# Moving the value steps, the gated biases and the output stores of a quantised cross-attention kernel, and cutting its scale loads into eight

## The chip, the core and the metric

The kernel runs on one core of a Trainium2 chip. The metric is device time in microseconds for one execution. Engines in the views: PE (matrix products), PEld (its weight loads), DVE (vector), ACT (scalar), POOL (GpSimd) and SP, which computes nothing here and issues most DMAs. An engine works through its instructions in order; so does SP through the DMAs that it issues.

## What is computed

A gated cross-attention block and a gated feed-forward block, with quantised arithmetic (rounding left out here):

```python
def xattn(x, cond):                      # 2048 query tokens, 4096 keys, C = 512, 16 heads of 32
    q = (x @ Wq + bq) * scale            # per head; integers of 8 bits, a step for each token and head
    k, v = split(cond @ Wkv + bkv)       # k: a step for each key and head; v: one step for each column
    attn = softmax(q @ k.T)              # then 8 bits, a step for each row
    return (attn @ v) @ Wp + bp
x = x + tanh(g_xattn) * xattn(layernorm(x), ctx)
x = x + tanh(g_ffn) * ffn(layernorm(x))  # 512 -> 2048 -> 512, ternary weights, 8-bit tokens, + b1, + b2
```

A value's step belongs to a column of `v`, which is a column of a head's output; it may be applied to the values, to the output of the head, or to the rows of `Wp` that this output meets. A bias `bp` times `tanh(g_xattn)` can be added to `x` before the product is.

## The kernel before, in words

There are three stretches. The first, the projections, makes integers of queries, keys and the first group of values, and leaves them and the key scales in DRAM (`q4d`, `k4d`, `skd`). It runs over 48 tiles of 128 rows; `extra[i]` holds what is done beside tile `i` (the ternary weights, the gates by `gates`, `tg1` and `tg2`).

The second, the attention, has 256 steps: 16 heads of 16 query tiles, the last two heads interleaved by four tiles. A step `i` has three chunks of keys (1536, 1536, 1024). PE makes the scores of a chunk (L726), DVE multiplies them by the key scales `skb` of the head and keeps their maximum (L735); POOL joins the maxima and makes a bias (L750, L752); ACT makes the exponentials as bytes in one of three buffers `r` (L755); SP transposes the bytes by DMA into `pT` (L769); POOL turns them into numbers that PE can read (L789, two casts a step); PE multiplies them by the values (L805); every four steps ACT empties the accumulator into `o` (L816) and issues the store of it to DRAM (L817). The score buffers are three until step 237 and two from there on, since the third holds then the output weight `wp_sb` and the vectors `bp` and `b2` (`load_for_ffn`).

Order is written out by hand. `plan[i, n]` lists what is issued after chunk `n` of step `i`; at the end of step `i` SP gets the transpose of step `i - 2` and then the loads of the next head. A head's data come in eight pieces (`load_piece`): 0 and 1 are the keys (L256), 2 and 3 the key scales in halves of 2048 keys, broadcast to 128 partitions, 1 MB each (L249), 4 to 7 the queries (L256). Before, pieces 0 to 7 of head `h + 1` are issued at the even steps of head `h`, and in head 0 at the steps `LATE`. Three more groups of values are made beside the heads (`plan_group`, from steps 3, 64 and 129): products from `cTd` (L646, L652, L661), stores and fetches by `vtd` (L674, L678), then transposes by DMA (L278). `value_scale` makes the steps `sv` of a group.

The third stretch is the output projection and the feed-forward block over tiles of 128 tokens. Its first tiles are started inside the last heads by `at_unit(i, n, ...)`: `projection_step` multiplies the output weight by the value steps (L282), `vector_for_ffn` the vectors by the gates (L191), `bias_x` adds the gated `bp` to the tokens (L1005), `wide_step` spreads the softmax steps (L1018), `first_project` multiplies (L1408). All of L191, L282 and L1005 is on POOL.

Of the kernel before, what the change touches and what calls it, by code (L numbers as in the profile page):

```python
# [11 lines left out]
F32 = mybir.dt.float32  # L12
# [5 lines left out]
AF = mybir.ActivationFunctionType  # L18
ALU = mybir.AluOpType
# [4 lines left out]
P = 128  # L24
# [5 lines left out]
INT_STEP = 2.0**-24  # L30
# [3 lines left out]
def flamingo_kernel(  # L34
# [31 lines left out]
    nc = tc.nc  # L66
    x = x.flatten_outer_dims()
    cond = cond.flatten_outer_dims()
    out = out.flatten_outer_dims()
    NQ, C = x.shape  # L70
    NK = cond.shape[0]
    H, HD = 16, 32
    INNER = w1.shape[0]
    QT, KT, CC, IC = NQ // P, NK // P, C // P, INNER // P
    HPG = P // HD
# [3 lines left out]
    def row(v, width):  # L79
        return v.rearrange("(a w) -> a w", a=1).broadcast_to([P, width])  # L80
# [79 lines left out]
    }  # L160
    b1r = third[:, at_vecs + 8 * C : at_vecs + 8 * C + 2 * INNER].bitcast(BF16)
    b1d = dram.tile([3, INNER], BF16, name="b1d")

    def load_b1(pool):
        bf = pool.tile([IC, P], F32, name="bf", bufs=1)
# [11 lines left out]

    def load_for_ffn():
        nc.sync.dma_start(wp_sb, wp.rearrange("(c p) n -> p c n", p=P))
        for name, v in (("bp", bp), ("b2", b2)):  # L180
            nc.sync.dma_start(vecs[name], row(v, C))
        for r in range(2):
            for a in range(3):
                at = r * HD + 3 * a
                nc.sync.dma_start(
                    b1r[at : at + 3, :].rearrange("p (m n w) -> p m n w", n=2, w=512)[:, :, r, :],
                    b1d.rearrange("p (m n w) -> p m n w", n=2, w=512)[:, :, r, :],
                )

    def vector_for_ffn(name, tg):  # L190
        nc.gpsimd.tensor_scalar(vecs[name], vecs[name], tg, 0.0, ALU.mult, ALU.add)  # L191

    def key_tile(n):

# [44 lines left out]
    def load_piece(h, n):  # L239
# [17 lines left out]
            dst[:, :, a : a + KB], src[a : a + KB, h * P : (h + 1) * P]  # L257
        )

    def value_scale(g, vmx):  # L260

        nc.vector.tensor_reduce(
            sv[:, g : g + 1], vmx, AX.X, ALU.max, apply_absolute_value=True
        )
        nc.vector.tensor_scalar(
            sv[:, g : g + 1], sv[:, g : g + 1], 1.0 / 127.0, 1e-8, ALU.mult, ALU.max
        )
        nc.vector.reciprocal(isv[:, g : g + 1], sv[:, g : g + 1])
# [8 lines left out]
            vqs[g] = vqp.tile([P, KT, P], F16, name="vq")  # L277
        nc.sync.dma_start_transpose(vqs[g][:, j * VB : (j + 1) * VB, :], vh)  # L278

    def projection_step(g):  # L280

        nc.gpsimd.tensor_scalar(  # L282
            wp_sb[:, g, :], wp_sb[:, g, :], sv[:, g : g + 1], 1.0 / INT_STEP, ALU.mult, ALU.mult
        )

    def integers(pool, f, scale):

# [21 lines left out]
    with tc.tile_pool(name="pw", bufs=1) as pw, tc.tile_pool(  # L309
# [215 lines left out]
            partial(nc.sync.dma_start, bq_sb, row(bq, C)),  # L525
        ]
        extra[5].append(load_gates)
        extra[45].append(gates)
        extra[4] += [partial(nc.vector.tensor_scalar, bq_sb, bq_sb, QSCALE, None, ALU.mult)]
        for j in range(8):  # L530
            extra[6 + 2 * j].append(partial(piece_load, j))
# [9 lines left out]

        extra[22].append(ffn_load)
        extra[23].append(lambda: parts_of_b1(pieces.pop(0), wr))
        LASTK = KT + QT - END - 1
        for k, n in ((-6, 0), (-3, 4), (-1, 5), (1, 1), (1, 2), (1, 3)):
            extra[LASTK + k].append(partial(load_piece, 0, n))
# [82 lines left out]

    VW = 256  # L630
    NV = NK // VW
    LATE = (4, 6, 8, 10, 11, 12, 13, 14)
    VALUES = {3: (1, 4, 2), 64: (2, 66, 0), 129: (3, 131, 0)}

    def plan_group(g, u0, dense):
        wv_g = wvs.next()
        vmx = fs.tile([P, KT // VB], F32, name="vmx")
        state = {}

        def start(j):  # L640
# [27 lines left out]

        def store(b):
            v = state.pop(("v", b))  # L670
            nc.vector.tensor_reduce(
                vmx[:, b : b + 1], v, AX.X, ALU.max, apply_absolute_value=True
            )
            nc.sync.dma_start(vtd[g][:, b * VB * P : (b + 1) * VB * P], v)  # L674

        def fetch(j):
            vt = vts.next()
            nc.sync.dma_start(vt, vtd[g][:, j * VB * P : (j + 1) * VB * P])  # L678
            state["vt", j] = vt

        def integer(j):
            state["vi", j] = value_integers(vis.next(), g, state.pop(("vt", j)))

        def cast(j):
            state["vh", j] = vhs.next()
            nc.vector.tensor_copy(state["vh", j], state.pop(("vi", j)))

        def turn(j):
            values_by_key(state.pop(("vh", j)), g, j)

        nc.sync.dma_start(wv_g, values_weight(g))
        load(0)
        for j in range(NV):
            u = start(j)
            v = start(j + 1) - 1
            for c, place in enumerate(((u, 2), (u + 1, 0), (v, 0) if v > u + 1 else (v, 1), (v, 2))):
                plan[place].append(partial(product, j, c))
            if j + 1 < NV:
                plan[u, 1].append(partial(load, j + 1))
            plan[v, 2].append(partial(leave, j))  # L700
            if (j + 1) * VW % (VB * P) == 0:
                plan[v + 1, 1].append(partial(store, j * VW // (VB * P)))
        u = start(NV)
        plan[u + 1, 0].append(partial(value_scale, g, vmx))
        for j in range(KT // VB):
            n = u - 1 + 2 * j
            plan[n + 1, 1].append(partial(fetch, j))
            plan[n + 3, 0].append(partial(integer, j))
            plan[n + 4, 2].append(partial(cast, j))
            plan[n + 5, 1].append(partial(turn, j))  # L710
# [65 lines left out]
    def plan_values(i, h, tg):  # L776
# [36 lines left out]

        def leave():
            o = ar.tile([P, P], F32, name="o", bufs=2)
            nc.scalar.copy(o, acc)  # L816
            nc.scalar.dma_start(  # L817
                ods[tg][h * HD : (h + 1) * HD, :].rearrange("d (c q) -> c d q", c=TG), o
            )

# [170 lines left out]
        return range(g * GT, (g + 1) * GT)  # L991

    def load_x(t):
        nc.sync.dma_start(X[t], x[t * P : (t + 1) * P, :])

    def load_o(t):
        o = fm["o"].next()
# [16 lines left out]
    def wide_step(t):  # L1014

        step_w = fm["step_w"].next()
        step = ff.pop(("step", t))
        nc.scalar.copy(step_w, step.unsqueeze(2).to_broadcast([P, H, HD]))  # L1018
        ff["step_w", t] = step_w

    def bias_y(g):
# [374 lines left out]
    def at_unit(i, n, *fs_):  # L1396
        plan[i, n].extend(fs_)
# [5 lines left out]
    def first_project(t, n):  # L1403
# [6 lines left out]
            start=(k == 0), stop=(k == NG - 1),  # L1410
        )

    for j in range(8):
        a = j * INNER // 8
        at_unit(
            199 + 3 * j, 1,
            partial(
                nc.sync.dma_start_transpose,
                w1T[:, :, a : a + INNER // 8],
                w1q[a : a + INNER // 8, :],  # L1420
            ),
        )
    at_unit(TWO + 2, 0, load_for_ffn)
    at_unit(TWO + 3, 2, partial(vector_for_ffn, "bp", tg1))
    for g in range(NG):
        at_unit(TWO + 4 + g // 2, 1, partial(projection_step, g))
    at_unit(TWO + 7, 1, partial(vector_for_ffn, "b2", tg2))
    at_unit(
        TWO + 7, 1,
        partial(  # L1430
# [5 lines left out]
    for t in range(2):  # L1436
        at_unit(240, t, partial(load_x, t))
        at_unit(241, 1, partial(load_o, t))
        at_unit(242 + t, 0, partial(bias_x, t))
    at_unit(241, 0, partial(steps_x, 0))  # L1440
    for t, u in ((0, 242), (1, 248)):
        at_unit(u - 1, 2, partial(wide_step, t))
# [15 lines left out]
    with tc.manual_schedule():  # L1458
        nc.vector.memset(less, -128.0 * INT_STEP)
        nc.vector.memset(ones_h, 1.0)  # L1460
        for i in range(len(steps)):
            h, t = steps[i]
            for n in range(len(CHUNKS)):
                scores(i, n)

                if n == 0 and i in VALUES:
                    plan_group(*VALUES[i])
                if n == 0 and i:
                    exps(i - 1)
                for run in plan.pop((i, n), ()):  # L1470
                    run()
            if i > 1:
                turn_exps(i - 2)
            if h == 0:
                if t in LATE:
                    load_piece(1, LATE.index(t))
            elif h + 2 < H and t % 2 == 0:
                load_piece(h + 1, t // 2)
            if 0 <= i - PAIR < TG:
                for n in ((0, 4, 2), (1, 3), (5,), (6, 7))[i - PAIR]:  # L1480
                    load_piece(H - 1, n)
# [142 lines left out]
```

## Time and profile before

| | us |
|---|---|
| median of three runs (lowest, highest) | 1709.2 (1708.43, 1712.97) |
| the profiled execution: own time | 1714.34 |
| the profiled execution: span of its instructions | 1712.5 |
| busy: DVE / PE / ACT / POOL | 1566.7 / 1366.1 / 1343.1 / 1283.7 |
| L735 on DVE, 768 instructions | 806.0 + 362.6 |
| L789 on POOL, 506 casts | 944.1 |
| L755 on ACT, 256 exponentials | 673.1 + 300.3 |
| first and last L735 start | 236.7 and 1452.8 |

Times are counted from the start of the span. In a timeline a line has the start, the duration, the engine with its line number, the operation and the tile written and read; a bracket gives the idle time before it and what ended that. "SPq" and "ACTq" are the queues that issue DMAs: the duration is that of the issue, not of the transfer. In a list of waits the numbers are the sum, the count and the longest. Idle time of an engine that is not the bottleneck costs nothing.

### The profile page before, as it was taken

What the parts mean: (1) busy time and instruction counts of PE and PEld (TensorE: products, weight loads), DVE (VectorE), ACT (ScalarE), POOL (GpSimd) and SP (SyncE); (2) the same over time, 40 slices, a digit from 0 to 9 for tenths busy, and PEclk for the clock granted to TensorE, in tenths of its full rate; (3) what the DMA queues carried; (4) which work ended last, traced back from release to release, by engine and by line L of the source; (5) the groups of instructions that cost most, each with busy time, mean ns of one, the idle gap of its engine ahead of it and who ended that gap; (6) DMA issues with size and microseconds to landing.
All of it is one profiled execution on the core that took longest, in us unless ns stands there. A gap on an engine that the chain in (4) does not pass through costs nothing. (4 is left out here: it accounts for less than half of the span.)

```text
span 1712.5 us, 31561 instructions
## 1 busy us (share of the span) xinstructions
PE 1366.1 (80%) x12174; PEld 592.1 (35%) x12174; DVE 1566.7 (91%) x2205; ACT 1343.1 (78%) x988; POOL 1283.7 (75%) x1315
## 2 busy tenths in 40 slices
PE   8999968889966899886678998766666577789986
PEld 4444423333322333332233333222222233434432
DVE  5787889999999999999989999999999989578998
ACT  2443468888889798888978888898887877679987
POOL 0001226889999899999988999999999998656645
PEclk9999975555555555555555556555555555889998
DMA  6767969999999999999999999989999776613325
GB/s 208 274 248 249 300 189 225 194 211 212 181 200 189 212 189 207 208 197 202 173 208 185 227 181 215 202 171 198 165 198 179 151 140 130 169 50 87 89 53 117
DMA packets 736331, 315.92 MB, mean 184 GB/s; under 512 B 658034, under 2 KB 703670, under 8 KB 729782
## 3 DMA queue, kind: packets, MB, share of 16 engines
q1 hardware_dynamic: 727414, 309.19, 83.4%
q10 hardware_dynamic: 8736, 4.72, 1.1%
q8 instruction: 95, 1.56, 0.4%
q14 instruction: 54, 0.44, 0.1%
q0 software_dynamic: 32, 0.01, 0.0%
HBM read 110.15 MB, written 40.12 MB: 88 GB/s over the span
## 5 line engine op out<-in xcount | busy, mean ns | idle before, releaser
L789 POOL CAST rT<-pT 128x2048 int16<-128x2048 uint8 x506 | 944.1, 1892 | 28.9 <-DMA pT<-r 7.5
L735 DVE CUSTOM_DVE_ANT_0 s<-ps_s,skb 128x1536 f32<-128x1536 f32 x531 | 806.0, 1574 | 21.1 <-PE ps_s L726 13.0
L755 ACT ACTIVATE r<-s,nb,sq 128x4096 uint8<-128x4096 f32 x177 | 673.1, 3803 | 135.6 <-POOL nb L752 77.1
L726 PE MATMUL ps_s<-kT,qT 32*128 32x512 bf16 x2048 | 463.7, 593 | 245.7 <-DVE m L735 232.1
L735 DVE CUSTOM_DVE_ANT_0 third<-ps_s,skb 128x1536 f32<-128x1536 f32 (+1 forms) x237 | 362.6, 1574 | 5.5 <-PE ps_s L726 3.2
L755 ACT ACTIVATE r<-third,nb,sq 128x4096 uint8<-128x4096 f32 x79 | 300.3, 3802 | 46.7 <-POOL nb L752 34.0
L726 PEld LDWEIGHTS <-qT 32*128 32x128 bf16 x2048 | 95.4, 99 | 578.0 <-issue 571.1
L805 PE MATMUL acc<-rT,vq 128*32 128x128 f16 x8192 | 265.1, 307 | 33.3 <-ACT o L816 25.2
L805 PEld LDWEIGHTS <-vq 128*32 128x32 f16 x8192 | 196.8, 137 | 147.0 <-issue 105.1
L652 PE MATMUL vacc<-fx 128*128 128x256 f32 x384 | 231.4, 706 | 7.7 <-ACT fx L661 6.7
L750 POOL TENSOR_SCALAR m<-m 128x1 f32<-128x1 f32 x256 | 91.8, 359 | 67.8 <-DVE m L735 61.2
L472 POOL TENSOR_SCALAR nsq<-sq 128x16 f32<-128x16 f32 x16 | 3.2, 203 | 171.9 <-DVE sq L291 171.9
L652 PEld LDWEIGHTS vacc<-fx 128*128 128x128 f32 x384 | 94.9, 306 | 91.3 <-issue 79.2
L431 PE MATMUL kacc<-wk_sb,cT 128*128 128x512 f32 x256 | 117.7, 603 | 0.0
L752 POOL TENSOR_SCALAR nb<-m,nsq 128x1 f32<-128x1 f32 x256 | 67.8, 265 | 23.9
L1117 PE MATMUL ph<-fx,skb 128*128 128x512 bf16 x256 | 64.2, 396 | 0.1
L431 PEld LDWEIGHTS kacc<-wk_sb,cT 128*128 128x128 f32 x256 | 47.1, 194 | 47.6 <-issue 47.0
L735 DVE DVE_READ_ACCUMULATOR2_ANT m<- 128x1 f32 x768 | 62.7, 82 | 0.0
L431 PE MATMUL qacc<-wq_sb,xT 128*128 128x512 f32 x128 | 59.4, 608 | 0.1
L460 DVE TENSOR_TENSOR f<-kacc,bk_sb 128x512 f32<-128x512 f32 x32 | 22.0, 689 | 31.1 <-PE kacc L431 30.1
L300 ACT COPY cT<-tr 128x512 f32<-128x512 f32 x32 | 18.6, 580 | 34.8 <-PE tr L299 34.6
L360 POOL TENSOR_SCALAR wi<-wt 128x512 bf16<-128x512 int32 (+1 forms) x32 | 21.7, 704 | 31.5 <-ACT wt L356 19.3
(233 smaller groups left out, 1370.1 us busy)
## 6 DMA issues: line engine op xcount, KB each, us to landing
skb<-skd SPq DMA_DIRECT2D x32, 1024.0 KB
fx<-cTd SPq DMA_DIRECT2D x48, 512.0 KB
wt<-in_L_ffn_w_dram SPq DMA_DIRECT2D x16, 1024.0 KB
in<-in_ctx_dram SPq DMA_DIRECT2D x32, 256.0 KB
cTd<-cT SPq DMA_DIRECT2D x8, 1024.0 KB
q4d<-rows4q SPq DMA_DIRECT2D x16, 512.0 KB
vtd<-fx SPq DMA_DIRECT2D x24, 256.0 KB
fx<-vtd SPq DMA_DIRECT2D x24, 256.0 KB
```

The lines of the kernel that those rows point to most:

```text
L360: nc.gpsimd.tensor_scalar(wi[:, a : a + w4], wt.bitcast(I32)[:, a : a + w4], 1.0, -1.0, ALU.min, ALU.max)
L431: nc.tensor.matmul(acc, tT[:, c, :], wk_sb[c] if kind == "k" else wq_sb[:, c, :], start=(c == 0), stop=(c == CC - 1),)
L460: nc.vector.tensor_tensor(f, acc, bk_sb, ALU.add)
L652: nc.tensor.matmul(state["acc"], wv_g[:, c, :], state["cT", j][:, c, :], start=(c == 0), stop=(c == CC - 1),)
L726: nc.tensor.matmul(ps_s[:, b * KB - k0 : (b + 1) * KB - k0], qT[rows, 0, t * P : (t + 1) * P], kT[rows, 0, a * KB : (a + 1) * KB], start=True,
L735: nc.vector.tensor_tensor_reduce(s[:, k0 : k0 + w], ps_s[:, :w], skb[:, k0 : k0 + w], 1.0, -3.0e38, ALU.mult, ALU.max, m3[:, n : n + 1],)
L750: nc.gpsimd.tensor_scalar(m, m3[:, 0:1], m3[:, 1:2], m3[:, 2:3], ALU.max, ALU.max)
L752: nc.gpsimd.tensor_scalar(nb, m, nsq[:, t, h : h + 1], LN255, ALU.mult, ALU.add)
L755: nc.scalar.activation(r.rearrange("p (n two) -> p two n", two=2), s.rearrange("p (two n) -> p two n", two=2), AF.Exp, bias=nb, scale=sq[: ...
L789: cast(spreads[k][:, 2 * u : 2 * u + 2, :, :] .bitcast(I16) .rearrange("p a (two b) q -> p a two (b q)", two=2), pTs[u][:, :, k * NW : (k ...
L805: nc.tensor.matmul(acc[c * HD : (c + 1) * HD, :], vq[:, kb, h % HPG * HD : (h % HPG + 1) * HD], rT[:, c, b, :], start=(k == 0 and b == 0), ...
L1117: nc.tensor.matmul(ph[:, n, :], xqT[:, c, tok], w1T[:, c, at : at + 512], start=(c == 0), stop=False,)
```

## The change

Five things are done.

1. The steps of the values no longer go into the output weight (`projection_step` is gone). They are stored to `svd` and loaded as a column for each head into `svr`, by one store and four loads for each of the four groups, and `leave` applies them when ACT empties the accumulator. The constant `1 / INT_STEP` goes into `wide_step`.
2. The products of `bp` and `b2` with the gates, and the sum of the first two tiles of tokens with the gated `bp`, are made on POOL in the projections and kept in DRAM (`gbd`, `xbd`); `load_for_ffn` and `load_x` read those, and `vector_for_ffn` and two calls of `bias_x` are gone. The gates are made at tile 9 in place of tile 45.
3. The store of `o` is issued by SP at step `i + 9` for the first 13 heads, in place of ACT at step `i + 8`; for the last three it stays with ACT.
4. The key scales of a head come in eight loads of 512 keys (256 KB each).
5. These and the six other pieces are issued at steps 0 to 11 of a head (`PIECES_AT`, `SCALES_AT`), in head 0 at steps 4 to 15. The loads of the last head are unchanged.

```diff
+    gbd = dram.tile([2, C], F32, name="gbd")
+    xbd = dram.tile([2 * P, C], F32, name="xbd")
...
     def load_for_ffn():
         nc.sync.dma_start(wp_sb, wp.rearrange("(c p) n -> p c n", p=P))
-        for name, v in (("bp", bp), ("b2", b2)):
-            nc.sync.dma_start(vecs[name], row(v, C))
+        for k, name in enumerate(("bp", "b2")):
+            nc.sync.dma_start(vecs[name], gbd[k : k + 1, :].broadcast_to([P, C]))
...
-    def vector_for_ffn(name, tg):
-        nc.gpsimd.tensor_scalar(vecs[name], vecs[name], tg, 0.0, ALU.mult, ALU.add)
...
+    def load_scales(h, k):
+        a = k * KB
+        nc.sync.dma_start(
+            heads[h][1][:, a : a + KB], skd[h : h + 1, a : a + KB].broadcast_to([P, KB])
+        )
...
-    def projection_step(g):
-        nc.gpsimd.tensor_scalar(
-            wp_sb[:, g, :], wp_sb[:, g, :], sv[:, g : g + 1], 1.0 / INT_STEP, ALU.mult, ALU.mult
-        )
+    svr = keep.tile([P, H], F32, name="svr")
+    svd = dram.tile([NG, P], F32, name="svd")
+
+    def store_scale(g):
+        nc.sync.dma_start(svd[g : g + 1, :].rearrange("a p -> p a"), sv[:, g : g + 1])
+
+    def load_scale(g):
+        for c in range(HPG):
+            nc.sync.dma_start(
+                svr[c * HD : (c + 1) * HD, g * HPG : (g + 1) * HPG],
+                svd[g : g + 1, :].rearrange("a (h d) -> (a d) h", d=HD),
+            )
...
-        extra[45].append(gates)
+        extra[9].append(gates)
...
+        def bias_load():
+            wt = wr.tile([P, INNER], F32, name="wt")
+            biased.append(wt)
+            for k, v in enumerate((x[:P, :], x[P : 2 * P, :], row(bp, C), row(b2, C))):
+                nc.sync.dma_start(wt[:, k * C : (k + 1) * C], v)
+
+        def bias_steps():
+            wt = biased[0]
+            for k, tg in ((2, tg1), (3, tg2)):
+                b_k = wt[:, k * C : (k + 1) * C]
+                nc.gpsimd.tensor_scalar(b_k, b_k, tg, 0.0, ALU.mult, ALU.add)
+            for k in range(2):
+                for a in range(0, C, P):
+                    x_k = wt[:, k * C + a : k * C + a + P]
+                    nc.gpsimd.tensor_tensor(x_k, x_k, wt[:, 2 * C + a : 2 * C + a + P], ALU.add)
+
+        def bias_store():
...
+        for k, f in ((21, bias_load), (22, bias_steps), (24, bias_store)):
+            extra[k].append(f)
...
-    LATE = (4, 6, 8, 10, 11, 12, 13, 14)
+    LATE_HEADS = (H - 3) * QT
+    PIECES_AT = {0: (0,), 2: (1,), 4: (4,), 6: (5,), 8: (6,), 10: (7,)}
+    SCALES_AT = {1: (0,), 3: (1,), 5: (2,), 7: (3,), 9: (4, 5), 10: (6,), 11: (7,)}
...
         plan[u + 1, 0].append(partial(value_scale, g, vmx))
+        plan[u + 2, 2].append(partial(store_scale, g))
+        plan[u + 5, 2].append(partial(load_scale, g))
...
         def leave():
             o = ar.tile([P, P], F32, name="o", bufs=2)
-            nc.scalar.copy(o, acc)
-            nc.scalar.dma_start(
+            nc.scalar.activation(o, acc, AF.Identity, scale=svr[:, h : h + 1])
+            if i < LATE_HEADS:
+                plan[i + 9, 2].append(partial(send, o, nc.sync))
+            else:
+                send(o, nc.scalar)
+
+        def send(o, eng):
+            eng.dma_start(
                 ods[tg][h * HD : (h + 1) * HD, :].rearrange("d (c q) -> c d q", c=TG), o
             )
...
     def load_x(t):
-        nc.sync.dma_start(X[t], x[t * P : (t + 1) * P, :])
+        src = xbd if t < 2 else x
+        nc.sync.dma_start(X[t], src[t * P : (t + 1) * P, :])
...
-        nc.scalar.copy(step_w, step.unsqueeze(2).to_broadcast([P, H, HD]))
+        nc.scalar.activation(
+            step_w, step.unsqueeze(2).to_broadcast([P, H, HD]), AF.Copy, scale=1.0 / INT_STEP
+        )
...
+    at_unit(5, 2, partial(store_scale, 0))
+    at_unit(8, 0, partial(load_scale, 0))
...
-    at_unit(TWO + 3, 2, partial(vector_for_ffn, "bp", tg1))
-    for g in range(NG):
-        at_unit(TWO + 4 + g // 2, 1, partial(projection_step, g))
-    at_unit(TWO + 7, 1, partial(vector_for_ffn, "b2", tg2))
...
-        at_unit(242 + t, 0, partial(bias_x, t))
...
-            if h == 0:
-                if t in LATE:
-                    load_piece(1, LATE.index(t))
-            elif h + 2 < H and t % 2 == 0:
-                load_piece(h + 1, t // 2)
+            if h + 2 < H:
+                for n in PIECES_AT.get(t if h else t - 4, ()):
+                    load_piece(h + 1, n)
+                for k in SCALES_AT.get(t if h else t - 4, ()):
+                    load_scales(h + 1, k)
```

More of the change, by code (lines that the diff above doesn't have):

```diff
@@ L543, in flamingo_kernel @@
         extra[23].append(lambda: parts_of_b1(pieces.pop(0), wr))
+        biased = []
+        def bias_load():
[13 more added lines that the diff above has]
+        def bias_store():
+            wt = biased.pop()
+            nc.sync.dma_start(
+                xbd.rearrange("(a p) c -> p a c", p=P),
+                wt[:, : 2 * C].rearrange("p (a c) -> p a c", c=C),
+            )
+            nc.sync.dma_start(
+                gbd.rearrange("(a k) c -> a k c", a=1),
+                wt[:1, 2 * C :].rearrange("p (a c) -> p a c", c=C),
+            )
+        for k, f in ((21, bias_load), (22, bias_steps), (24, bias_store)):
+            extra[k].append(f)
         LASTK = KT + QT - END - 1
@@ L1017, in wide_step @@
         step = ff.pop(("step", t))
-        nc.scalar.copy(step_w, step.unsqueeze(2).to_broadcast([P, H, HD]))
+        nc.scalar.activation(
+            step_w, step.unsqueeze(2).to_broadcast([P, H, HD]), AF.Copy, scale=1.0 / INT_STEP
+        )
         ff["step_w", t] = step_w
```

## The prediction

> **What bounds the kernel now.** I read the stretch table first, cut at the heads' borders: every head is 16 steps, and a step turns 128 queries against 4096 keys. Columns: window, its length, then busy time (and count) of PE, weight loads, DVE, ACT, POOL, then PE clock, DMA share, GB/s.
>
> ```profile
> 539.90:618.70 78.80, 64.19 (x677) 27.54 (x675) 74.38 (x102) 64.65 (x42) 69.38 (x64) 0.50 1.02 207
> 842.60:924.50 81.90, 63.49 (x676) 27.03 (x673) 75.43 (x102) 66.06 (x45) 69.64 (x64) 0.50 0.99 199
> 924.50:1072.80 148.30, 129.99 (x1365) 56.76 (x1365) 147.67 (x200) 128.63 (x80) 138.85 (x128) 0.55 1.03 203
> 1072.80:1292.00 219.20, 139.15 (x1928) 58.27 (x1928) 219.05 (x301) 194.04 (x119) 208.67 (x194) 0.50 0.97 186
> 1367.00:1401.10 34.10, 25.00 (x259) 10.84 (x258) 28.45 (x41) 24.16 (x15) 32.91 (x34) 0.50 0.76 144
> ```
>
> DVE is the bound: in heads 11 to 13 (1072.8 to 1292.0) it lacks 0.15 us. A step costs it two reads of 1536 scores and one of 1024, 1.68 + 1.68 + 1.14 = 4.50 us from start to start in its timeline, and none of that is touched. Only idle DVE can be won. By the same table it is 3.0 us in head 0, 2.8 in head 1, 4.4 in head 4, 6.5 in head 8 (together 16.7), 2.6 in the other heads up to 13, and 2.7, 5.7 and 2.8 in 1292 to 1367, 1367 to 1401 and 1401 to 1454.
>
> Second, the timeline of SP, which issues the loads and the transposes, in head 3 (start, duration, what):
>
> ```profile
> 498.70 0.57 SPq L249 DMA_DIRECT2D skb<-skd  x1
> 499.37 5.64 SPq L769 DMA_TRANSPOSE pT<-r  x1
> 505.10 1.22 SPq L278 DMA_TRANSPOSE vq<-fx  x1
> 506.41 0.53 SPq L678 DMA_DIRECT2D fx<-vtd  x1
> 507.04 3.01 SPq L769 DMA_TRANSPOSE pT<-r  x1
> 510.10 1.25 SPq L256 DMA_TRANSPOSE qT<-q4d  x1
> 511.45 1.96 SPq L769 DMA_TRANSPOSE pT<-r  x1
> ```
>
> A copy is issued in about 0.5 us, but the transpose behind it holds SP longer: 5.64 us after 1 MB of scales, 3.01 after a 256 KB fetch, 1.96 after neither. Third, what that does in head 4, in the timelines of ACT, PE and DVE, and the waits of the attention stretch (237 to 1300):
>
> ```profile
> 577.53 3.80 ACT L755 ACTIVATE r<-s,nb,sq 128x4096 uint8<-128x4096 f32 x1 [4.26 <-DMA pT<-r]
> ```
>
> ```profile
> 582.08 1.05 PE L805 MATMUL acc<-rT,vq 128*32 128x128 f16 x32 [4.66 <-ACT o L816]
> ```
>
> ```profile
> 583.71 1.23 DVE L735 CUSTOM_DVE_ANT_0 s<-ps_s,skb 128x1024 f32<-128x1024 f32 x1 [1.21 <-PE ps_s L726]
> ```
>
> ```profile
> ACT r L755 <- DMA pT<-r: 52.5, 27, 4.3
> ```
>
> The chain: 1 MB in the queue, a late transpose, an exponential without a free `r` buffer, PE in order behind an accumulator that ACT has not emptied, DVE idle. ACT waits 52.5 us so, but DVE feels it only in heads 0, 1, 4 and 8.
>
> Fourth, POOL and ACT near the end of the scores:
>
> ```profile
> 1376.85 1.36 POOL L282 TENSOR_SCALAR third<-third,sv 128x512 f32<-128x512 f32 x2
> ...
> 1379.00 1.28 POOL L1005 TENSOR_TENSOR vq<-vq,third 128x512 f32<-128x512 f32 x1
> 1380.23 3.72 POOL L789 CAST rT<-pT 128x2048 int16<-128x2048 uint8 x2
> 1383.95 1.35 POOL L282 TENSOR_SCALAR third<-third,sv 128x512 f32<-128x512 f32 x2
> ...
> 1386.08 1.28 POOL L1005 TENSOR_TENSOR vq<-vq,third 128x512 f32<-128x512 f32 x1
> ```
>
> ```profile
> 1386.03 3.80 ACT L755 ACTIVATE r<-s,nb,sq 128x4096 uint8<-128x4096 f32 x1 [3.19 <-POOL nb L752]
> ```
>
> POOL's own step (maximum, bias, two casts) is also 4.50 us, so whatever is added to it delays the next bias, the exponential and, with two score buffers from step 237 on, DVE.
>
> **The sum, part by part.** I sum against the profiled execution: span 1712.5, own time 1714.34 us. That time stands 5.1 above the median 1709.2, so a difference found on it is taken from the median.
>
> *POOL work gone from 1367 to 1406.* Two vectors by the gates at 0.69 (L191), four slices of the output weight at 0.69 (L282), two token biases at 1.28 (L1005): 1.38 + 2.74 + 2.56 = 6.7 us. From the maximum at 1367.21 to that at 1405.79 POOL makes 7 steps in 38.6 us where 7 x 4.50 are 31.5; the excess is 7.1. What is late next: DVE's reciprocal and product (0.25 + 0.6), one PE wait on the wide step (0.46), and the two-buffer wait that steps 237 to 240 show without any added POOL work (0.28 to 0.36 every other step, 1.3 in 7). Sum 2.6, so the gain is 7.1 - 2.6 = 4.5 (2.5 if more falls to PE or ACT; 6.7 if all counts).
>
> *Scales in eight loads.* Per head two 1 MB loads at 0.57 + (5.64 - 1.96) = 4.2 us of queue, 8.5 in all, become eight of 256 KB. Nearest row: the 256 KB fetch, 0.53 + (3.01 - 1.96) = 1.6, so 12.6 at most. At least: a queue that lags issues the copy beside the transpose before it. The cycle from 505.10 to the next such transpose at 513.50 takes 8.40; two pairs of a small and a large transpose without a copy, read in head 0 at 304.40 to 308.1, are 2 x 3.75; the fetch is 0.9, eight are 7.2. So -1.3 to +4.1 us per head, and I take the low end where it matters, because the heads that stall are those that lag. Spread over twelve steps, no single load holds a transpose for 5.6 us. Heads 0, 1, 4 and 8 have 16.7 us idle, of which I leave 0.4 per head for the short PE pauses that heads 9 and 10 show too (0.6 in two): at most 15. The stalling heads are also short of queue as a whole (SP's issues fill 72.9 of 78.8 us in head 4 and 79.5 of 81.9 in head 8, 68.0 of 74.2 in head 5, my sums of its rows), which spreading doesn't mend. I take a third: gain 5 (0 to 15).
>
> The Trainium skill speaks against this part: its page DMA: Bandwidth & Descriptors asks for DMAs of 1 MiB or more (section Bandwidth) and fits 2.0 us fixed plus bytes over 436 GB/s to one that GpSimd issues (section Anatomy of one DMA). An estimate from that page: 8.8 us become 20.8 per head, 168 over fourteen heads; with the 6 us of free queue per head, some 80 us slower. The trace's 0.9 to 1.6 per 256 KB stands against its 2.6.
>
> *Output stores on SP; steps of the values.* 52 of the 64 stores (heads 0 to 12) leave ACT, 0.53 us each, and are issued by SP before a transpose. SP now waits there for ACT's emptying of the accumulator, which comes 0.25 us after the exponential that the next transpose needs anyway. Nearest row: the 256 KB store L674, 0.53 plus some 0.4 that the next transpose is longer; four per head are 3.7 at most, 2 at least. Behind it on SP stand the transpose, then the head's loads; ACT waits for both. Four times per kernel come one store and four loads of a column of steps, five issues at 0.5, 2.5 us plus a landing, at steps 5 to 8 and near heads 3, 7 and 11. The free 6 us per head cover this in most heads; in heads 0, 3/4 and 7/8 cover is gone. Against it ACT saves 0.67 us (issue and gap) per store, which helps just where ACT is late. The scaled emptying itself costs ACT some 0.08 more than the 0.244 copy (from the 0.454 of a 128x256 Identity and the 0.708 of a 128x512 one), under ACT's idle seventh. Cost 2 (-2 to +10).
>
> *Head 0's late scales.* Its loads end at step 15: keys 3584 to 4095 of head 1 are asked for behind the transpose that starts at 314.43 and lasts until 318.3 (start of the second of the pair), while DVE reads them 3.4 us into head 1, at 316.9. Unlagged it would be in time. Once, 1 us (0 to 4.6).
>
> *The projections (0 to 237).* PE is busy 223.5 of 236.7, POOL 28.6, ACT 94.2. POOL gets 2 x 0.69 + 8 x about 0.35, SP four loads and two stores, 1.5 MB at 0.74 DMA share. The Tanh moves between two square roots: two more table loads (1.28 each) on an ACT that is 40% busy, one of them perhaps ahead of the first exponential. Cost 0.5 (0 to 2.6). Loads of the premade rows and of the biased vectors replace loads of equal size, and the wide step's scale rides on an existing instruction: 0. The last 258 us run unchanged.
>
> Sum: -4.5 - 5 + 2 + 1 + 0.5 = -6.0. The profiled 1714.3 becomes 1708.3, the median 1709.2 becomes 1703.2.
>
> **The rivals.** *Only the end moves* (0.28): the stalls of heads 4 and 8 are a shortage of queue, and spreading brings nothing: -4.5 + 2 + 0.5 = -2, 1707. For it: the 72.9 and 79.5 us of issues. *The queue becomes the bound* (0.22), slower: with 1.6 us per quarter load and 0.9 per store a head needs 12.6 + 3.7 - 8.5 = 7.8 us more of SP where about 6 are free. Place: heads 0 to 11; it decides from 1.3 us per quarter load on (8 x 1.3 + 3.7 - 8.5 = 5.6). Overflow is 1.8 in an ordinary head, twice, four or five in heads 0, 4 and 8 that have least free: about 7 x 0.5 (some shed as the lag grows) + 3 x 3 = 12; 12 - 4.5 + 0.5 = +8, 1717. Against it: a lagging queue issues copies for nothing. *Every stall goes* (0.12): -15 - 4.5 + 1.5 = -18, 1691. That the products come out elsewhere than stated isn't open: the removed lines are on POOL in the rows above.
>
> **How the numbers follow.** Forecast 0.38 (1697 to 1704). Faster by over 0.3% (5.1 us, about what a measurement of this kernel can tell from no change) is below 1704.1: 0.38 + 0.12 = 0.50. Within 0.3%: 0.28. Slower: 0.22. The range reaches from 1694, which leaves out half of the case in which all stalls go, to 1716, which leaves out about half of the slower one.
>
> **What would show it.** No L191 or L282 on POOL after 1300 and the wait of ACT for POOL's bias there under 1 us; ACT's wait for transposes under 52.5 us, no transpose above 4.5 us behind a scale load; DVE idle in heads 4 and 8 down to some 7 us together. Wrong would be: transposes that wait longer in ordinary heads (5, 6, 9, 10) with new DVE idle there, a gap of several us at the start of head 1, or a longer stretch before the first scores.

## The result, and the profile after

The changed kernel takes 1775.53 us (median of 4 runs, 1775.11 to 1777.37) against 1710.85 for the kernel before on the same chip: the ratio is 1.0381, 95% interval 1.0362 to 1.0399. It is 64.7 us slower. The forecast was 1703.2, in a range of 1694 to 1716. The profiled execution took 1777.37 us, its span is 1775.6.

I cut the changed trace at the same borders as the one before, by DVE's first score of each head. The stretch ahead of the first score is 236.7 us before and 235.8 after; the stretch behind the last step's start is 264.9 and 265.1; steps 240 to 246 take 38.6 and 36.2. From the first score to step 240 it is 1130.3 before and 1196.7 after: +66.4, more than the whole loss.

The stretch table, for heads 4, 8, 9 and 10, 11 to 13, and the first steps of the last pair (window, its length, then busy time and count of PE, weight loads, DVE, ACT, POOL; PE clock, DMA share, GB/s):

```profile
561.80:646.40 84.60, 60.78 (x674) 26.64 (x675) 74.67 (x100) 67.21 (x43) 69.54 (x64) 0.54 1.02 193
884.40:968.50 84.10, 62.15 (x672) 26.70 (x673) 74.77 (x102) 67.13 (x43) 69.69 (x65) 0.50 0.99 192
968.50:1122.10 153.60, 135.00 (x1369) 57.57 (x1369) 148.29 (x198) 127.45 (x82) 137.43 (x128) 0.50 0.97 196
1122.10:1355.30 233.20, 137.99 (x1928) 57.70 (x1928) 221.37 (x299) 196.03 (x119) 210.95 (x194) 0.50 0.94 175
1432.50:1464.20 31.70, 23.33 (x255) 10.28 (x255) 28.34 (x41) 24.25 (x15) 26.60 (x26) 0.50 0.80 155
```

DVE's work is what it was (148.29 us in heads 9 and 10 against 147.67); the windows around it are longer. Heads 11 to 13, where DVE lacked 0.15 us before, now lack 11.8, and heads 9 and 10 lack 5.3 where it was 0.6. So the loss is no longer a matter of a few heads: heads 0 to 14 lose 6.3, 6.4, 4.6, 5.5, 5.8, 2.7, 6.3, 5.1, 2.2, 4.0, 1.3, 9.3, 3.0, 1.6 and 2.2.

SP's timeline at the end of head 10 shows the new order in the transposes' queue (start, duration, line, what):

```profile
1104.84 0.57 SPq L261 DMA_DIRECT2D skb<-skd  x1
1105.52 3.01 SPq L817 DMA_TRANSPOSE pT<-r  x1
1108.57 0.58 SPq L261 DMA_DIRECT2D skb<-skd  x1
1109.25 0.58 SPq L871 DMA_DIRECT2D od<-o  x1
1109.93 3.95 SPq L817 DMA_TRANSPOSE pT<-r  x1
1113.97 0.54 SPq L720 DMA_DIRECT2D vtd<-fx  x1
1114.61 0.55 SPq L692 DMA_DIRECT2D fx<-cTd  x1
1115.22 8.87 SPq L817 DMA_TRANSPOSE pT<-r  x3
```

Each of the first three transposes has one or two copies just ahead of it. What follows is the chain of the kernel before, now in a head that had none. In the timelines of ACT, PE and DVE, with the idle time and its releaser in brackets:

```profile
1116.10 3.81 ACT L803 ACTIVATE r<-third,nb,sq 128x4096 uint8<-128x4096 f32 x1 [1.74 <-DMA pT<-r]
...
1122.14 3.80 ACT L803 ACTIVATE r<-s,nb,sq 128x4096 uint8<-128x4096 f32 x1 [2.14 <-DMA pT<-r]
```

```profile
1126.70 1.05 PE L853 MATMUL acc<-rT,vq 128*32 128x128 f16 x32 [4.02 <-ACT o L864]
```

```profile
1128.33 1.23 DVE L783 CUSTOM_DVE_ANT_0 third<-ps_s,skb 128x1024 f32<-128x1024 f32 x1 [2.80 <-PE ps_s L774]
```

ACT twice lacks a free `r` buffer, because the transpose that empties it is late; it comes late to the full accumulator; PE, in order, stands 4.02 us in front of that accumulator with the next scores behind it; DVE is idle for 2.80. The sums for the attention stretch (236 to 1363 here; total, times, longest):

```profile
ACT r L803 <- DMA pT<-r: 127.3, 69, 5.6
...
PE acc L853 <- ACT o L864: 67.4, 34, 5.0
```

The first was 52.5 us in 27 waits; I had given its fall as the sign of a right forecast.

Head 1's start has the gap that the forecast named as a sign against it. SP's timeline, then DVE's:

```profile
321.99 1.47 SPq L261 DMA_DIRECT2D skb<-skd  x1
323.56 3.00 SPq L817 DMA_TRANSPOSE pT<-r  x1
326.61 0.58 SPq L261 DMA_DIRECT2D skb<-skd  x1
327.29 0.59 SPq L871 DMA_DIRECT2D od<-o  x1
```

```profile
330.87 1.23 DVE L783 CUSTOM_DVE_ANT_0 s<-ps_s,skb 128x1024 f32<-128x1024 f32 x1 [8.47 <-DMA skb<-skd]
```

The load of the last 512 scales starts at 326.61, 4.2 us after DVE wanted them at 322.40, and DVE waits 8.47 us.

At the end of the scores POOL is rid of the moved work, as forecast, and ACT's wait for its bias is shorter, 1.74 us here (3.19 at the same step before) and 0.95, 1.52 and 1.01 at the next three; the sign that it falls below 1 us is met in one of the four:

```profile
1449.31 3.80 ACT L803 ACTIVATE r<-s,nb,sq 128x4096 uint8<-128x4096 f32 x1 [1.74 <-POOL nb L800]
```

### The profile page after: what moved, and what is told of

It reads as the page before. It is cut to its first block, busy times and chain, and to the rows that moved or that the text cites. A ratio compares the mean times of both kernels' runs of the same rounds, so it can differ in the third digit from the quotient of the medians.

```text
span 1775.6 us, 31747 instructions
## 1 busy us (share of the span) xinstructions
PE 1345.5 (76%) x12174; PEld 585.8 (33%) x12174; DVE 1572.7 (89%) x2205; ACT 1349.3 (76%) x990; POOL 1283.3 (72%) x1317
## 4 chain that ended last, share of the span: by engine, by line
POOL 24%; DVE 16%; issue 9%; DMA 9%; ACT 8%; PE 5%; SPq 2%; ACTq 0%; POOLq 0%; DVEq 0%
POOL rT L837 16%; DMA pT<-r 8%; DVE s L783 8%; ACT r L803 5%; DVE third L783 3%; POOL m L798 2%; SPq L817 1%; POOL nb L800 1%; PE ps_s L774 1%; PE ph L1174 1%; PE acc L853 1%; DVE s L1222 1%; DVE s L1229 1%; PE vacc L1465 1%; DMA fx<-cTd 1%
## 5 line engine op out<-in xcount | busy, mean ns | idle before, releaser
L774 PE MATMUL ps_s<-kT,qT 32*128 32x512 bf16 x2048 | 453.5, 584 | 257.2 <-DVE m L783 242.8
L853 PE MATMUL acc<-rT,vq 128*32 128x128 f16 x8192 | 260.8, 304 | 86.6 <-ACT o L864 71.4
L698 PE MATMUL vacc<-fx 128*128 128x256 f32 x384 | 226.7, 692 | 25.2 <-ACT fx L707 24.4
L800 POOL TENSOR_SCALAR nb<-m,nsq 128x1 f32<-128x1 f32 x256 | 68.4, 267 | 23.9
```

The costliest lines, as they stand in the source:

```text
L698: nc.tensor.matmul(state["acc"], wv_g[:, c, :], state["cT", j][:, c, :], start=(c == 0), stop=(c == CC - 1),)
L774: nc.tensor.matmul(ps_s[:, b * KB - k0 : (b + 1) * KB - k0], qT[rows, 0, t * P : (t + 1) * P], kT[rows, 0, a * KB : (a + 1) * KB], start=True,
L800: nc.gpsimd.tensor_scalar(nb, m, nsq[:, t, h : h + 1], LN255, ALU.mult, ALU.add)
L853: nc.tensor.matmul(acc[c * HD : (c + 1) * HD, :], vq[:, kb, h % HPG * HD : (h % HPG + 1) * HD], rT[:, c, b, :], start=(k == 0 and b == 0), ...
```

## The experiments

Fifteen kernels were run. Each result is given against the kernel before of its own group of runs (medians 1710.81, 1710.77, 1709.96 and 1710.38), with the 95% interval of the ratio.

**Which part costs what.** The first three kernels split the change. `e1_scales` has the eight loads alone:

```
+ PIECES_AT, SCALES_AT, load_scales as in the change
- if h == 0: ... load_piece(1, LATE.index(t))  ...
+ for k in SCALES_AT.get(t if h else t - 4, ()): load_scales(h + 1, k)
```

> The kernel before with one part of the change alone: the head scales in eight 256 KB loads, at the changed steps. Three theories of the +65 us. Count: every copy put between SP's transposes holds the next transpose until it has landed; from the changed trace a 256 KB load costs 0.58 + (3.01 - 1.96) = 1.6 us of queue and a store 0.58 + (2.87 - 1.96) = 1.5. Then eight loads for two are 12.8 - 8.5 = +4.3 us per head against some 6 free: only heads 0, 4 and 8 overflow and head 1 starts late (about 8), 1722 (1715 to 1735), and the two parts together cost more than the sum of each alone. Coupling: the stores make SP wait for ACT, the loads are harmless: 1710 to 1716. Schedule: the loads crowded into twelve steps, the last one of head 0 too late, make the loss: 1750 or more.

Measured: 1741.11, +30.3 (1.0181, 1.0159 to 1.0203). That lies between the three theories: more than the price of the loads by my table, less than the whole loss. DVE's gap at the start of head 1 is 6.80 us here.

`e2_stores` has the stores alone:

```
  nc.scalar.copy(o, acc)
- nc.scalar.dma_start(ods[tg]..., o)
+ if i < LATE_HEADS: plan[i + 9, 2].append(partial(send, o, nc.sync))
+ else: send(o, nc.scalar)
```

> The kernel before with the output stores of heads 0 to 12 on SP ahead of the transpose, nothing else (ACT empties the accumulator by a plain copy, as before). Count: four stores at 1.5 us are +6.0 us per head against some 6 free: 1720 (1712 to 1735), the loss in heads 0, 4 and 8. Coupling (a store at the head of the queue waits for an ACT that is late, and holds the transpose that this ACT needs next): most of the loss is here, 1745 to 1770, with SP's wait on ACT in front of L817's stores growing with the lag. Schedule: 1710 to 1714.

Measured: 1726.24, +15.4 (1.0078, 1.0055 to 1.0102). Count holds better than coupling. Heads 3, 5, 6, 7, 9 and 10 are within 0.5 us of before; head 8 loses 5.2, head 4 4.0, head 12 2.3, head 1 2.2. So the free queue does cover four stores, in the heads that have it.

`e3_rest` has neither, but all the rest of the change:

```
- for k in SCALES_AT...: load_scales(h + 1, k)
+ if h == 0: ... load_piece(1, LATE.index(t)) ...
- if i < LATE_HEADS: plan[i + 9, 2].append(partial(send, o, nc.sync)) ...
+ send(o, nc.scalar)
```

> The changed kernel with its loads and stores put back as before: two 1 MB scale loads per head at the old steps, every output store on ACT's queue. What stays is the value steps applied as the accumulator is emptied, the five small copies per group that carry them, and the biases made in the projections. All theories: the scores as before, steps 240 to 246 2 to 4 us shorter, projections 0 to 1 shorter: 1706 (1703 to 1710). If it stands above 1715, the small copies of the steps or the scaled emptying have a part in the loss, which none of the three theories has.

Measured: 1730.27, +19.5 (1.0109, 1.0090 to 1.0127). None of the three theories has this. The three parts together make 30.3 + 15.4 + 19.5 = 65.2, the whole loss. By the profiled executions 19.5 of the 22.6 us that are added between the first score and step 240 lie in heads 0, 3, 7 and 11, where the columns of value steps are stored and loaded. SP's and ACT's timelines in head 0:

```profile
262.38 0.53 SPq L289 DMA_DIRECT2D svd<-sv  x1
263.01 1.93 SPq L816 DMA_TRANSPOSE pT<-r  x1
264.99 1.01 SPq L691 DMA_DIRECT2D fx<-cTd  x1
266.06 8.34 SPq L816 DMA_TRANSPOSE pT<-r  x1
```

```profile
273.14 3.80 ACT L802 ACTIVATE r<-s,nb,sq 128x4096 uint8<-128x4096 f32 x1 [5.83 <-DMA pT<-r]
```

The store of 128 steps, 512 bytes in all, is issued in 0.53 us and by the trace lands at 270.57, 8.2 us later; the transpose issued behind it lands at 273.04, and the one after that holds SP for 8.34 us.

**The small copies.** `e5_spread_pe` replaces the five small copies per group:

```
- nc.sync.dma_start(svd[g : g + 1, :]..., sv[:, g : g + 1])     (and the four loads)
+ for a in range(HPG): for c in range(HPG):
+     nc.tensor.matmul(ps_v[c*HD:(c+1)*HD, a:a+1], ident[:, a*HD:(a+1)*HD],
+                      sv[:, g:g+1], start=True, stop=True, tile_position=(0, c*HD))
+ nc.vector.tensor_copy(svr[:, g*HPG:(g+1)*HPG], ps_v)
```

> The kernel of run e3_rest with its five small copies per group of heads (one store of a column of 128 steps, 4 bytes a row, and four loads of it) taken out: sixteen one-column products with the identity place the steps in PSUM, and one small copy by DVE takes them out. The scaled emptying and the premade biases stay. If the small copies made the loss of e3_rest (its heads 0, 3, 7 and 11, where they lie, are 6.9, 2.8, 6.6 and 3.3 us longer than before, 19.6 of it; the store that is issued at 262.38 lands at 270.57): 1707 (1703 to 1711). If the scaled emptying or the moved Tanh made it: still 1725 to 1732.

Measured: 1708.17 (10 runs), 0.9985 (0.9972 to 0.9997), 2.6 us faster than before. The small copies make all of e3's loss: 19.5 + 2.6 = 22.1 us for twenty copies. The copy out of PSUM that replaces them takes DVE 0.157 us, four times. ACT's wait for transposes is 43.0 us in this trace. This version beats both kernels, by little.

`e9_row_store` changes the shape of the store, and for the first group also its place, by two chunks:

```
+ nc.tensor.matmul(ps_v, sv[:, g : g + 1], ident, start=True, stop=True)
+ nc.vector.tensor_copy(svt, ps_v)
- nc.sync.dma_start(svd[g : g + 1, :].rearrange("a p -> p a"), sv[:, g : g + 1])
+ nc.sync.dma_start(svd[g : g + 1, :], svt)
```

> The kernel of run e3_rest with only the store of the steps changed in shape: one product with the identity turns the column of 128 steps into a row, DVE copies it out, and the store writes 512 bytes from one partition instead of 4 bytes from each of 128; the four loads of 4-byte pieces stay as they are. If it is the store that costs (8.2 us to land, the transpose behind it late): 1711 (1707 to 1715), near e5_spread_pe's 1708. If the loads cost as much: 1720; if they cost all: 1730.

Measured: 1722.12, +12.2 (1.0076, 1.0055 to 1.0097). SP's timeline shows the store at half the issue time, and by the trace it lands 1.8 us later (8.2 to 11.3 in the four places of e3_rest, 1.1 to 1.8 here):

```profile
267.47 0.25 SPq L293 DMA_DIRECT2D svd<-svt  x1
267.78 0.55 SPq L695 DMA_DIRECT2D fx<-cTd  x1
268.38 3.69 SPq L820 DMA_TRANSPOSE pT<-r  x1
```

So the changed store is 7 us of the 22, and 15 remain with the store's place and the four loads. In the profiled executions head 0, where the store's place moved too, gives back 5.0; heads 3, 7 and 11 give back 4.1 together, so the shape alone has a share, but not surely all of the 7. `e14_wide_loads` cuts the number of the loads' pieces to a quarter:

```
- svd[g : g + 1, :].rearrange("a (h d) -> (a d) h", d=HD)
+ svd[g : g + 1, :].rearrange("a (d h) -> (a d) h", d=HD)      (the row stored in that order)
```

> The kernel of run e9_row_store (1722) with the row of steps stored in another order, so that each of the four loads takes 32 pieces of 16 bytes instead of 128 of 4. Presence of four more copies: 1718 to 1722, no gain. Pieces: most of the 14 us above e5_spread_pe goes, 1709 to 1714.

Measured: 1722.37, +12.0 (1.0070, 1.0043 to 1.0096): no gain. The pieces of the loads don't matter here. That the loads' mere presence costs the rest is what is left; no run takes out the loads alone.

**What a copy pays for.** `e4_groups` has eight loads in two places:

```
  if n in (2, 3):
+     w = NK // 2 if h in (0, H - 1) else KB
+     for a in range((n - 2) * NK // 2, (n - 1) * NK // 2, w): nc.sync.dma_start(skb[:, a : a + w], ...)
```

> The kernel before with each 1 MB scale load of heads 1 to 14 cut into four of 256 KB issued one after another at the old place (eight loads per head, but only two places). Count of copies: +4.3 us per head as with the spread loads, so like e1 without the late start of head 1, 1715 (1711 to 1725). Count of places (what is paid is a landing ahead of a transpose, not an issue): two places as before, plus 6 x 0.58 = 3.5 us of issues per head that the free 6 us hold: 1710 to 1715. Schedule: as before, 1710.

Measured: 1725.95, +15.1 (1.0086, 1.0068 to 1.0103).

`e6_sixteen` has them in eight places, with no step that has two:

```
+ PIECES_AT = {0: (0,), 2: (1,), 8: (4,), 10: (5,), 12: (6,), 14: (7,)}
+ SCALES_AT = {1: (0,), 3: (1,), 4: (2,), 5: (3,), 6: (4,), 7: (5,), 9: (6,), 11: (7,)}   (head 1 as before)
```

> The kernel before with eight 256 KB scale loads in heads 2 to 14, spread with the six other pieces over the steps 0 to 14, one piece in a step; head 1's pieces as before (two 1 MB loads). Against e1_scales (1741) it has the same count of loads, no late last piece for head 1 (6.7 us of e1's gap) and no step with two scale loads. Count of loads: as e4_groups, 1726 (1720 to 1730). Count of places at which a transpose finds a copy ahead of it: 1732 to 1740, above e4_groups. Crowding in twelve steps: 1710 to 1718.

Measured: 1725.93, +15.2 (1.0088, 1.0068 to 1.0107). The two agree: eight loads cost the same in two places as in eight. What they share is the number of copies. Crowding into fewer steps costs more, as `e11_head1_old` below shows.

`e13_row_loads` adds copies that carry next to nothing:

```
+ if 0 < h + 1 < H - 1 and t in (1, 3, 5, 7, 9, 11):
+     row1 = ar.tile([1, P], F32, name="row1", bufs=1)
+     nc.sync.dma_start(row1, skd[h : h + 1, t * P : (t + 1) * P])
```

> The kernel before with six added loads per head (heads 0 to 13, steps 1, 3, 5, 7, 9, 11), each of one row of 512 bytes into a buffer that nothing reads. Presence (every copy between transposes costs an issue and a landing, whatever its size): as the six more loads of e4_groups and e6_sixteen, 1726 (1720 to 1732). Pieces and bytes (a 256 KB load is 128 rows): six issues of some 0.3 and a landing of some 1 us in the free queue, 1711 to 1715.

Measured: 1724.09, +13.7 (1.0069, 1.0043 to 1.0096). Six copies of 512 bytes cost what six more copies of scales cost. In SP's timeline:

```profile
657.29 0.38 SPq L1481 DMA_DIRECT2D row<-skd  x1
658.05 2.95 SPq L769 DMA_TRANSPOSE pT<-r  x1
```

The table that follows comes from SP's rows between 237 and 1300. It gives the median time for which a transpose of `r` holds SP, by what was issued since the one before it:

| issued since | median hold, us | in kernel |
|---|---|---|
| nothing (it follows a transpose of `r` directly) | 2.92, 2.82, 1.99 | before, e13, after |
| a transpose of `qT` | 1.95 to 2.04 | before, e13, after |
| one row of 512 bytes | 2.71 | e13_row_loads |
| one store of 64 KB | 2.87 | after |
| one load of 256 KB | 3.01 | after |
| a load of 256 KB and a store | 3.40 | after |
| four loads of 256 KB | 4.33 | e4_groups |
| one load of 1 MB | 5.28 | before |
| one load of 2 MB | 7.69 | e10_one_load |

Against the row behind `qT` a copy costs, with its own issue, 0.4 + (2.71 - 1.95) = 1.2 us if it is nearly empty and 0.58 + (3.01 - 1.96) = 1.6 at 256 KB; at 1 MB and 2 MB size shows. But these are prices at one place. Against a transpose that follows another of `r` directly, the same 512 bytes cost 0.4 + (2.71 - 2.82) = 0.3. The sum of all of SP's issues from the first score to step 224 (960.8 us before) tells more: it grows by 30.8 us for the 84 rows of e13_row_loads, 0.37 each, and by 26.4 for the 52 stores of e2_stores, 0.51 each. For the scale loads it grows by 48.3 in e1_scales, 45.1 in e6_sixteen and 23.9 in e4_groups, that is 3.5, 3.5 and 1.7 per head in which they are issued. These sums scatter: e5_spread_pe, without an added copy, is 15.8 below before. So the table's prices are too high, for the small copies by about a factor of three.

`e10_one_load` goes the other way, on e5_spread_pe:

```
- a = (n - 2) * NK // 2 ...  skb[:, a : a + NK // 2]        (n = 2 and 3)
+ w = NK ...                 skb[:, a : a + w]              (n = 2 alone, heads 1 to 14)
```

> The kernel of run e5_spread_pe with one 2 MB scale load per head (heads 1 to 14) at the place of the first 1 MB load. If the price goes by the number of copies (e4_groups: six more per head cost 15 us in all, 84 copies, 0.18 each after what the free queue absorbs): 14 copies fewer, 1704 to 1708, no slower than e5_spread_pe. If the longest hold of a single transpose decides (5.3 us after 1 MB, about 9 after 2 MB, two r buffers' worth): stalls of 3 to 4 us in most heads, 1730 to 1750.

Measured: 1714.36 (10 runs), 1.0030 (1.0015 to 1.0045): 7.0 us worse against before than e5_spread_pe. It is neither theory in full: fewer copies did not pay, and a hold of 7.7 us costs far less than I gave it. Of one, two and eight loads per head, the two of 1 MB are the best.

**The places.** `e11_head1_old` is e1_scales with head 1's pieces as before:

```
+ if h == 0:
+     if t in LATE: load_piece(1, LATE.index(t))
```

> The kernel of run e1_scales with head 1's pieces as before (two 1 MB loads at the old steps), the other heads' eight loads at the changed steps. Against e1_scales (1741) it takes away only the late last load of head 1: 1735 (1733 to 1738) if the 6.7 us gap at the start of head 1 was net loss, 1740 if the time comes back elsewhere in head 1. Against e6_sixteen (1726, the same counts spread over fifteen steps) it shows what the crowding of two or three copies into a step costs: 7 to 10.

Measured: 1734.95, +25.0 (1.0151, 1.0127 to 1.0176). The late load costs 30.3 - 25.0 = 5.3 us net, and the crowding into twelve steps 25.0 - 15.2 = 9.8.

`e8_stores_later` is e2_stores with each store two steps later:

```
- plan[i + 9, 2].append(partial(send, o, nc.sync))
+ plan[i + 11, 2].append(partial(send, o, nc.sync))
```

> The kernel of run e2_stores (output stores of heads 0 to 12 on SP) with each store two steps later, so that ACT has emptied the accumulator long before SP comes to the store. Coupling (SP waits there for a late ACT): the loss goes, 1711 to 1716. Place in the queue (each store is one more copy that must land ahead of the next transpose): as e2_stores, 1722 to 1730.

Measured: 1720.85, +10.1 (1.0060, 1.0037 to 1.0084). Both theories have a share: by the medians 5.3 of the 15.4 is SP waiting for ACT's emptying, 10.1 is four more copies per head in the queue. The trace of e2_stores has that wait, ten times before a store and 9.5 us in all, and the trace of e8_stores_later has none. The size of the two shares is rough, since the runs overlap (1722.23 to 1728.01 and 1718.09 to 1723.99).

**Another queue.** `e7_act_loads` takes the 1 MB loads out of the transposes' queue:

```
- nc.sync.dma_start(skb[:, a : a + NK // 2], ...)
+ eng = nc.sync if h in (0, H - 1) else nc.scalar
+ eng.dma_start(skb[:, a : a + NK // 2], ...)
```

> The kernel before with the two 1 MB scale loads of heads 1 to 14 issued by ACT, at the same places in the program; sizes and counts unchanged. If the price of a copy is its place in the transposes' queue, 8.5 us per head leave SP's queue and the stalls of heads 0, 4 and 8 shrink: 1698 (1692 to 1705), with no transpose above 4 us behind nothing. If the price is the time of the DMA engines (busy share about 1.0 in every head), which another queue does not change: 1708 to 1713, and the transposes still take about as long around the loads. ACT's own cost is 28 issues at about 0.6.

Measured: 1742.89, +32.1 (1.0198, 1.0142 to 1.0253), worse than either theory. ACT's timeline in head 8:

```profile
867.54 0.39 ACTq L250 DMA_DIRECT2D skb<-skd  x1
...
886.28 3.80 ACT L756 ACTIVATE r<-s,nb,sq 128x4096 uint8<-128x4096 f32 x1 [14.90 <-DMA pT<-r]
```

By the trace the transpose issued by SP at 867.15 lands at 886.17 and the load issued by ACT at 867.54 lands at 885.67, each some 18 to 19 us after its issue. In the kernel before, a 1 MB load issued by SP at 281.39 and the transpose issued behind it have both landed by 290.85, 9.5 us later. This pair is the worst of 28: the load's median landing is 7.3 us against 6.2 before. But 12 transposes of `r` between 237 and 1300 land more than 12 us after their issue, where none did before (the longest was 10.3). What makes them long these runs don't show. The Trainium skill's page DMA: Bandwidth & Descriptors (section Rules for kernel authors) says that spreading DMAs over the issuing engines brings no bandwidth because they share the same 16 DMA engines. This run agrees, and goes further: it costs 32 us here.

**Do the prices hold in the changed kernel?** `e12_after_pe` takes the small copies out of it, `e15_after_act` puts the stores back on ACT, by the same edits as in e5_spread_pe and e3_rest.

> The changed kernel with its five small copies per group replaced by products with the identity, as in e5_spread_pe; eight loads and stores on SP stay. If the parts' costs add up (e1_scales +30.3, e2_stores +15.4, small copies 1730.3 - 1708.2 = 22.1, sum with the end's gain +65): 1775.5 - 22.1 = 1753 (1749 to 1757). If a crowded queue makes each copy dearer, more than 22 comes back: 1740 to 1748. If the small copies only fill stalls that the others make anyway: 1760 or more.

Measured: 1757.62, +47.7 (1.0287, 1.0259 to 1.0315): 17.0 of the 64.7 come back.

> The changed kernel with all output stores on ACT's queue as before. Additive: 1775.5 - 15.4 = 1760 (1756 to 1764). A store costs more in a fuller queue: 1745 to 1755. In a fuller queue the stores hide behind stalls that the loads make: 1765 or more.

Measured: 1760.44, +50.1 (1.0291, 1.0263 to 1.0318): 14.6 come back, against 15.4 on the kernel before. The parts add up, to within some 5 us.

## Why the prediction was wrong

Point by point, by its own terms:

- *POOL work gone, -4.5.* Right in kind, too large: seven steps went from 38.6 to 36.2, 2.4 (35.5 in e5_spread_pe, 3.1). I let 2.6 of the excess of 7.1 stay; 4.0 to 4.7 stayed. With POOL free, DVE waits for PE in four of the seven steps (0.48, 0.83, 0.31 and 0.31), where I had counted one wait of 0.46, and 1.4 in the first two steps for ACT.
- *Scales in eight loads, -5.* This is the step that failed first, by sign. Measured: +30.3 alone. I had bounded a quarter load at 0.9 to 1.6 us of queue and took "the low end where it matters, because the heads that stall are those that lag", from pairs of rows in one lagging stretch. I took -1.3 to +4.1 us of queue per head, and counted on the low end; SP's issues grew by 3.5 per head in e1_scales, near the upper end. The low end, 0.9 for a load, rested on one pair of transposes (304.40 to 308.1), doubled. And I expected a third of the idle 16.7 us back from a shorter longest hold. Heads 4 and 8 give nothing back together: in e4_groups they are 4.4 and 0.3 us longer, in e6_sixteen 2.5 longer and 2.7 shorter. Of the 30.3, 15 is the number of copies, 9.8 the crowding into twelve steps, which I did not price at all, and 5.3 the late load.
- *Output stores and value steps, +2.* Two terms, both mis-sized. The stores cost 15.4. Their price in the queue was not the error: by the sum of SP's issues it is 0.51 us each, where I had 0.5 to 0.9. The error was to call it covered in most heads (heads 1, 4, 8 and 12 lose 2.2 to 5.2), and some 5.3 is for SP's wait on ACT, which I had named and put at nothing because the emptying "comes 0.25 us after the exponential". The columns of steps cost 17 to 22 where I had 2.5 us of issue per group "plus a landing". I priced five copies by their bytes; the store is 128 pieces of 4 bytes and takes 8.2 to 11.3 us to land, and the loads, as far as the runs tell, cost by being there.
- *"The free 6 us per head cover this in most heads."* True of the stores in heads 3, 5, 6, 7, 9 and 10 (e2_stores), false of the other parts: the scale loads alone cost heads 6 and 9 4.8 and 3.9 (e1_scales), the copies of the steps alone cost head 7 6.6 (e3_rest). Nor were the free 6 us used up: SP issues nothing for 3.4 to 8.6 us in each of heads 0 to 13 of e1_scales, and still 3.3 to 7.8 in the changed kernel. Free time summed over a head does not cover a copy that is late where it stands. Together the parts cost more than one by one in some heads (head 11: 9.3 against 5.0, head 5: 2.7 against -0.8) and less in others (head 8: 2.2 against 6.9, head 12: 3.0 against 8.4); in total they just add up.
- *Head 0's late scales, +1 (0 to 4.6).* The mechanism was right; the size was 8.47 us of gap and 5.3 net. I carried the unlagged time of that transpose over into a kernel in which the queue ahead of it is fuller.
- *Projections, +0.5.* No cost is seen: 236.7 became 235.8, and in the kernels that leave the projections alone the first score starts between 233.2 and 236.7. The scaled emptying takes 0.347 us against 0.244, near the 0.08 more that I gave it.

The rival that the queue becomes the bound was right on the direction and the resource. SP's issues grew by 84.0 us over heads 0 to 13, 6.0 a head, about the 6 that it needed. But a full queue is not the condition: e13_row_loads adds 2.2 a head, far from 6, and costs 13.7. Its size, +8, was wrong, since it let the overflow fall mainly on heads 0, 4 and 8 and left the crowding and the small copies out. The estimate from the Trainium skill's page, some 80 us slower by a fixed cost per DMA, stood much nearer to the result than my bounds from the rows, though the parts show that the page's sum, over the scale loads alone, is not what happened: they cost 30 of the 65. What the runs bear out is the page's point that a small copy is paid mostly in a fixed cost: six more copies per head cost the kernel 13.7 us with 512 bytes each and 15.1 with 256 KB.

What stays open: by the sums of SP's issues e4_groups adds 1.7 us of queue per head, e13_row_loads 2.2 and e6_sixteen 3.5, yet they cost 15, 14 and 15. So the sum of queue time does not order the three; all have six more copies per head. Why it is the number that counts, at the same places or not, and whatever a copy carries (its landing, or the change between transpose and copy), these runs do not tell apart.

## What to carry to other kernels

Where one queue feeds transposes back to back, price added copies by their number and not by their bytes: here some 80 of them cost 14 to 15 us, 0.16 to 0.19 us of the kernel each, with 512 bytes or 256 KB. Do not take the queue's free time in a head for cover: transposes came late and DVE stood idle while SP still had 3 to 8 us free in the same head. Look at the shape of a small transfer: a column of 128 values of 4 bytes was better spread by TensorE here than sent through DRAM. Moving a load to another engine's queue took it out of the order here, not out of the way.

## What was not expected of the hardware

A store of 4 bytes from each of 128 partitions took 8.2 to 11.3 us from issue to landing in e3_rest (6.3 to 9.4 in the changed kernel), and 1.1 to 1.8 as one row of 512 bytes in e9_row_store; the Trainium skill's page DMA: Bandwidth & Descriptors (section Specifications) gives 512 bytes as the smallest transfer at full rate, with a read-modify-write below, and these numbers agree in direction. With loads of 1 MB on ACT's queue beside transposes on SP's, the worst pair took 18 to 19 us each to land, and 12 transposes took over 12 us, where none did with all on SP's queue. 84 loads of 512 bytes cost the kernel 13.7 us, about what 84 more of 256 KB cost.
